# Layer 0's heads turned by DMA instead of TensorE, and a new order inside the period, in a two-layer graph kernel

## The chip, the cores and the metric

The kernel runs on one core of a Trainium2 chip. The time is the device time of one execution in microseconds (us); a kernel's time is the median of its runs. In the profile PE is TensorE (PEld its weight loads), DVE is VectorE, ACT is ScalarE, POOL is GpSimd and SP is SyncE, whose queue issues nearly all DMAs here. A line such as L522 is a line of the kernel's source.

## The reference

There are 64 independent graphs of 256 nodes with 512 features, and a mask `adj` per graph. Two residual layers of masked attention follow each other, each after a layer norm and a relu. Layer 0 has 8 heads and also keeps only pairs of nodes whose mapped features have a cosine over 0.1; layer 1 has 4 heads and an output product.

```python
# --- layer 0 (8 heads of 64) ---
h = relu(layernorm(x))
m = h @ map_w.T + map_b
n = m / |m|  per head                      # unit vectors
cos_adj = (n @ n.T) * ~adj > 0.1
q, k = m @ q_w.T + q_b, m @ k_w.T + k_b
p = softmax(where(adj, -1e10, q @ k.T / 8)) * keep     # keep: by node, ~adj[..., 0]
a = cos_adj * p
Ax = a @ (h @ gcn_map_w.T + gcn_map_b)
out = relu(Ax @ gcn_W.T / (a.sum(-1) + 1))
x = x + out
# --- layer 1 (4 heads of 64) ---
h = relu(layernorm(x))
q, k, v = h @ Wq, h @ Wk, h @ Wv
attn = softmax(where(adj, q @ k.T / 8, -max))
x = x + (attn @ v) @ Wo + bo
```

## The kernel before

The graphs run through a software pipeline. `period(i)` works on four graphs at once: on graph i (called `g`) it does layer 0's attention and the products of layer 1; on graph i-1 (`b`) layer 1's attention and the output; on graph i+1 (`nx`) the map, messages, queries and keys of layer 0; on graph i+2 (`n2`) the input norm and its transpose. On every engine the instructions stand in the order of the source. Inside a period the products are generators (`m` map, `s` messages, `q` queries, `k` keys, `j` layer 1's queries and keys, `v` its values), and each `next` puts one step of their matmuls into the order.

Products of 256-token blocks are made of seven block products each, from sums and differences of the blocks (`left_factors`, on POOL). Attention is kept transposed: scores have keys on partitions and queries along the row. Softmax numerators `e` are masked by DVE and halved into `d` by POOL; sums over keys are matmuls with ones. Layer 0's sums need one more thing: where a pair of nodes is far (`far`, the transposed upper block of cosines), e is set to zero by `far_back`. Layer 0's result `av` has features on partitions and tokens along the row, so it has to be turned before it is added to `x`: in `heads_back`, by eight transposes of TensorE (`p_l`). The input of the first layer is turned in another way: `sent` takes each fp32 number apart into two 16-bit halves, sends both through a DMA transpose (which moves 16-bit elements), and `join` puts the halves back together on ACT.

The helpers that the change touches, or that stand on the way between layer 0's heads and layer 1's norm:

```python
    def shifts(g, tag):

        deviations(g)
        g.shift = small.tile([P, NT], F32, tag="shift", name=f"shift{tag}")
        for t in range(NT):
            nc.scalar.activation(g.shift[:, t:t + 1], g.less[:, t:t + 1], AF.Copy, scale=g.rs[:, t:t + 1])
        g.flat = sb1.tile([P, NT, 2, D], U16, tag="kT", name=f"flat{tag}")
        g.turn = sb1.tile([P, 2, NKC, S], U16, tag="nT", name=f"turn{tag}")

    def sent(g, t):

        bits = g.xn.bitcast(U16).rearrange("p (d k) -> p k d", k=2)
        for k in range(2):
            nc.scalar.copy(g.flat[:, t, k, :], bits[:, k, :])
            nc.sync.dma_start_transpose(out=g.turn[:, k, :, t * P:(t + 1) * P], in_=g.flat[:, t, k, :])

    def join(g, k):
        nc.scalar.copy(g.bits[:, k], g.turn[:, k])

    def lengths(g, p):
        g.rn = sb1.tile([P, S], F32, tag="rn", name=f"rn{g.i}")
        nc.vector.tensor_scalar_max(g.rn, p, COS_EPS * COS_EPS)

    def by_head(rows, step, dst, name):

        n = P // step
        by = dram.tile([n // 2, 2, S], F32, tag=f"by{step}", name=f"by_{name}")
        nc.sync.dma_start(out=by.rearrange("c s q -> (c s) q"), in_=rows[::step, :])
        for s in range(2):
            nc.sync.dma_start(out=dst[s * DH:(s + 1) * DH], in_=by[None, :, s, :].to_broadcast([DH, n // 2, S]))

    def far_back(g, c):

        e = g.e[c][:, :, S:S + P]
        nc.vector.scalar_tensor_tensor(e, g.far[c], 0.0, e, op0=ALU.is_gt, op1=ALU.mult)

    def values(g, n):
        av = bank(f"av{g.i}_{n}")
        for c in (2 * n, 2 * n + 1):
            weighed(av, c - 2 * n, g.sem, g.e[c], 2 * c)
        nc.scalar.activation(g.avs[:, 2 * n:2 * n + 2, :], av, AF.Relu)

    def total(g, sm):
        g.homes = both_homes(g.i)
        g.sms = g.homes[:, 0, :]
        nc.scalar.activation(g.sms, sm, AF.Copy, accum_out=chk[:, g.i, 0:1])

    def sums_back(g):

        rt = bank(f"rt{g.i}", [P, NT, P])
        for t in range(NT):
            nc.tensor.transpose(rt[:, t, :], g.sms[:, t * P:(t + 1) * P], w.ident)
        r = small.tile([P, NT, 2, 4], F32, tag="r", name=f"r{g.i}", bufs=1)
        nc.vector.reciprocal(r, rt.rearrange("p t (k n) -> p t n k", n=32)[:, :, :2, :])
        rc = small.tile([P, NT, 2, 4], F32, tag="rc", name=f"rc{g.i}", bufs=1)
        nc.scalar.activation(rc, r, AF.Copy, accum_out=chk[:, g.i, 1:2])
        g.rk = small.tile([P, NT, H0], F32, tag="rk", name=f"rk{g.i}", bufs=1)
        for t in range(NT):
            nc.vector.tensor_scalar_mul(g.rk[:, t, :], r[:, t].rearrange("p n k -> p (n k)"), g.keep[:, t:t + 1])

    def heads_back(g):
        for t in range(NT):
            p = bank(f"p_l{g.i}_{t}", [P, NKC, P])
            for c in range(NKC):
                nc.tensor.transpose(p[:, c, :], g.avs[:, c, t * P:(t + 1) * P], w.ident)
            o = sb2.tile([P, H0, DH], F32, tag="xn", name=f"o{g.i}_{t}")
            nc.vector.tensor_mul(o, p.rearrange("p c (h d) -> p (c h) d", d=DH),
                                 g.rk[:, t, :, None].to_broadcast([P, H0, DH]))
            nc.gpsimd.tensor_add(g.xs[:, t, :], g.xs[:, t, :], o.rearrange("p h d -> p (h d)"))

    def own(b, home):
        own = sb1.tile([P, 2, NIC, S], F32, tag=home, name=f"own{b.i}")
        b.avs1, b.z = own[:, 0], own[:, 1]

    def sums1(b, parts):

        zb = bank(f"zb{b.i}", [P, S])
        for c in range(NIC):
            ps = parts(c)
            for j, part in enumerate(ps):
                for s in range(2):
                    h = 2 * c + s
                    nc.tensor.matmul(zb[32 * h:32 * (h + 1), :], w.ones[:, :32], part[:, s, :],
                                     start=(j == 0), stop=(j == len(ps) - 1))
        b.rz = sb1.tile([P, S], F32, tag="rz", name=f"rz{b.i}")
        nc.scalar.activation(b.rz, zb, AF.Copy, accum_out=chk[:, b.i, 2:3])

    def inverted(b):

        nc.vector.reciprocal(b.rz, b.rz)
        by_head(b.rz, 32, b.z, f"rz{b.i}")

    def divided(b):
        nc.vector.tensor_mul(b.avs1, b.avs1, b.z)
```

Of the pools: a `tag` names a buffer, and two tiles of one tag with `bufs=1` follow each other in the same memory. `avs`, `sq` and layer 1's `hT` share "wide"; the left factors have "sh"; `sem` has two buffers. All PSUM tiles come in turn from a ring of eight banks.

The period (`turned` makes p_t, `result` makes p_o):

```python
    def period(i):
        g, nx = graphs[i], graphs[i + 1]
        b, n2 = graphs.get(i - 1), graphs.get(i + 2)

        def off_edges(*cs):
            for c in cs:
                masked(g.e[c], g.mask, edges=False)

        def halved_sums(*cs):
            for c in cs:
                g.d[c] = halves(g.e[c], f"0_{i}_{c}")


        if b:
            b.e1 = [exps(products(b.k1T, b.q1T, c, f"sc1_{b.i}_{c}"), f"1_{b.i}_{c}") for c in range(NIC)]
        for c in range(NKC):
            g.e[c] = exps(products(g.kT, g.qT, c, f"sc0_{i}_{c}"), f"0_{i}_{c}")
        if b:
            for c in range(NIC):
                masked(b.e1[c], b.mask, edges=True)
        m, s = mapped(nx), messages(nx)
        next(m)
        next(s)

        off_edges(0, 1)
        halved_sums(1, 0)
        if b:
            b.d1 = [halves(b.e1[c], f"1_{b.i}_{c}") for c in range(NIC)]
        units(g)
        next(m)
        off_edges(2)
        halved_sums(2)
        next(m)
        next(s)
        next(m)

        for c in range(NKC):
            far_off(g, c, cosines(g, c))
            if c == 0:
                off_edges(3)
                halved(nx, lambda: halved_sums(3))
        for c in range(NKC):
            far_added(g, c, 0)
        if n2:
            shifts(n2, f"0_{n2.i}")
        q = queries(nx)
        next(q)
        next(s)
        if n2:
            scaled(n2, f"0_{n2.i}", 0)
        next(q)
        if n2:
            sent(n2, 0)
        squares(nx)
        next(s)
        if n2:
            scaled(n2, f"0_{n2.i}", 1)
            sent(n2, 1)
        for c in range(NKC):
            if c < 3:
                next((q, s, q)[c])
            far_back(g, c)
            far_added(g, c, 1)
        lengths(nx, norms(nx))

        if b:
            sums1(b, lambda c: [b.d1[c]])
            own(b, "qk1")
            inverted(b)
            nc.scalar.copy(b.avs1, values1(b))
        g.avs = sb1.tile([P, NKC, S], F32, tag="wide", name=f"avs{i}")
        values(g, 0)
        values(g, 1)
        total(g, sums(g, lambda c: [g.d[c]], "sm"))
        if n2:
            joined(n2, f"0_{n2.i}")
            join(n2, 0)
        k = keys(nx)
        next(k)
        if b:
            nc.scalar.activation(b.rz, b.rz, AF.Copy, accum_out=chk[:, b.i, 3:4])
        sums_back(g)
        heads_back(g)
        if n2:
            join(n2, 1)
        next(k)
        if n2:
            edges(n2, g.homes)
        if b:
            divided(b)
        moments(g, f"1_{i}")
        next(k)
        deviations(g)
        normalized(g, f"1_{i}")
        nc.scalar.activation(nx.rn, nx.rn, AF.Sqrt)

        nc.scalar.activation(spare[:, 1:], spare[:, :1], AF.Exp)
        if b:                                   # p_o
            for t in range(NT):
                result(b, t)
            nc.sync.dma_start(out=out_t[b.i], in_=b.xs)
        if i + 3 < B:
            graphs[i + 3] = load(i + 3)
        g.h1T = turned(g, f"1_{i}", "wide")
        j = queries_keys1(g)
        for t in range(NT):
            nc.gpsimd.tensor_add(g.xs[:, t, :], g.xs[:, t, :], w.bo_b)
        next(k)
        next(j)
        v = values_in(g)
        next(v)
        nc.vector.reciprocal(nx.rn, nx.rn)
        spread(nx)
        ...  # the other steps of j and v; left_factors of n2.hT; moments of graph i + 3
```

(Cut here: the loads, the general fallback kernel that is compiled but isn't entered with these inputs, the first graph's preparation, and `closing`, which treats the last two graphs without the pipeline and also calls `values`, `heads_back`, `sums1` and `inverted`.)

Of the kernel before, what the change touches and what calls it, by code (L numbers as in the profile page):

```python
# [150 lines left out]
def fast_path(ctx, tc, a, w, chk, out):  # L151
# [232 lines left out]
    def by_head(rows, step, dst, name):  # L384

        n = P // step
        by = dram.tile([n // 2, 2, S], F32, tag=f"by{step}", name=f"by_{name}")
        nc.sync.dma_start(out=by.rearrange("c s q -> (c s) q"), in_=rows[::step, :])
        for s in range(2):
            nc.sync.dma_start(out=dst[s * DH:(s + 1) * DH], in_=by[None, :, s, :].to_broadcast([DH, n // 2, S]))  # L390

    def spread(g):

        g.nT = sb1.tile([P, NKC, S], F32, tag="nT", name=f"nT{g.i}")
        by_head(g.rn, 16, g.nT, f"rn{g.i}")
# [109 lines left out]
    def sums_back(g):  # L505
# [85 lines left out]
    def sums1(b, parts):  # L591
# [26 lines left out]
    def period(i):  # L618
# [21 lines left out]
        next(s)  # L640

# [6 lines left out]
        off_edges(2)  # L648
        halved_sums(2)
# [33 lines left out]
        if b:  # L683
            sums1(b, lambda c: [b.d1[c]])
            own(b, "qk1")
            inverted(b)
            nc.scalar.copy(b.avs1, values1(b))
        g.avs = sb1.tile([P, NKC, S], F32, tag="wide", name=f"avs{i}")
        values(g, 0)
        values(g, 1)  # L690
        total(g, sums(g, lambda c: [g.d[c]], "sm"))
        if n2:
            joined(n2, f"0_{n2.i}")
            join(n2, 0)
# [5 lines left out]
        heads_back(g)  # L700
        if n2:
            join(n2, 1)
        next(k)
        if n2:
# [19 lines left out]
        g.h1T = turned(g, f"1_{i}", "wide")  # L724
        j = queries_keys1(g)
# [16 lines left out]
    def closing():  # L742
# [24 lines left out]
        values(g, 0)  # L767
        values(g, 1)
# [9 lines left out]
        if b:  # L778
            sums1(b, lambda c: both(b.e1[c]))
            own(b, "kT")  # L780
# [7 lines left out]
        if b:  # L788
            inverted(b)
        g.h1T = turned(g, f"1_{g.i}", "wide")  # L790
# [409 lines left out]
```

## Time and profile before

| | |
|---|---|
| time, median of 3 runs | 3622.2 us (3621.92 to 3622.47) |
| span in the profiled run | 3620.2 us |
| granted TensorE clock, mean | 0.998 |
| busy: PE, PEld | 3594.1 us (99%), 3133.2 us (87%) |
| busy: DVE, ACT, POOL | 2625.7 us (73%), 1971.2 us (54%), 2222.5 us (61%) |
| DMA | 191.65 MB in 359208 packets, mean 53 GB/s |
| p_l (L522), the transposes of layer 0's heads | 512 matmuls, 66.4 us busy |
| DMA transposes on SP: far, turn, mask | 256, 248, 128 |

Busy time is the time in which an engine had at least one instruction under way. Matmuls are pipelined, so the mean duration of one is longer than the distance between two; in a timeline, the difference of two starts tells what a group takes of the engine. A timeline line has the start, the duration, the engine, the source line, the operation, output and inputs, and the count; in brackets stands the idle time of the engine before it, with what ended that idle time. A line of waits has the total in us, how often it happened, and the longest. The chain of work that ended last is followed back from the last instruction, and its shares say which engine set the end.

### The profile page before, as it was taken

The page shows a single profiled execution, that of the slowest core. Times are in us where ns is not written, and L with a number is a line of the kernel's source. Part 1 is how long each engine was busy: PE and PEld are TensorE (multiplying, and loading weights), DVE is VectorE, ACT ScalarE, POOL GpSimd, SP SyncE. Part 2 cuts the span into 40 slices and gives each one's busy share as a digit, 9 for nine tenths or more (in the row PEclk, how much of TensorE's full clock was granted, in tenths as well). Part 3 has the DMA queues.
Part 4 walks back from the last instruction along what each step waited for, and adds up shares of the span by engine and source line. Part 5 has one row for each costly group of instructions (what it writes and reads, how often), then busy time and mean ns, then how long its engine had stood idle before and what let it go on. Part 6 is the DMA issues. An engine that isn't in the chain of part 4 may idle for free.

```text
span 3620.2 us, 79022 instructions
## 1 busy us (share of the span) xinstructions
PE 3594.1 (99%) x29945; PEld 3133.2 (87%) x29945; DVE 2625.7 (73%) x5549; ACT 1971.2 (54%) x4796; POOL 2222.5 (61%) x2044
## 2 busy tenths in 40 slices
PE   8999999999999999999999999999999999999998
PEld 7888888889888888888888988888889888888896
DVE  7777767777777777776777777767777777777776
ACT  4555555555555555555555555555555555555553
POOL 4656666566566665665656656666566566665662
PEclk9999999999999999999999999999999999999999
DMA  4121121212211212112122121121111211211111
GB/s 119 42 61 44 54 57 47 55 46 54 61 44 52 54 48 58 44 55 61 42 55 52 49 60 44 54 56 47 55 46 54 61 44 53 57 47 57 45 48 34
DMA packets 359208, 191.65 MB, mean 53 GB/s; under 512 B 270348, under 2 KB 325160, under 8 KB 358824
## 3 DMA queue, kind: packets, MB, share of 16 engines
q1 hardware_dynamic: 358088, 185.97, 19.4%
q8 instruction: 240, 3.93, 0.5%
q14 instruction: 144, 1.18, 0.1%
q10 hardware_dynamic: 544, 0.52, 0.0%
q0 software_dynamic: 192, 0.04, 0.0%
HBM read 94.41 MB, written 34.34 MB: 36 GB/s over the span
## 4 chain that ended last, share of the span: by engine, by line
PE 98%; DVE 1%; ACT 0%; issue 0%; DMA 0%; POOL 0%; SPq 0%; DVEq 0%; ACTq 0%; POOLq 0%
PE sc L416 10%; PE av L443 9%; PE p_m L287 7%; PE p_q L287 7%; PE p_k L287 7%; PE p_qk L287 6%; PE p_s L282 6%; PE p_o L615 6%; PE co L453 5%; PE p_qk_z L287 5%; PE p_m_z L287 5%; PE p_q_z L287 5%; PE p_k_z L287 5%; PE p_s_z L282 5%; PE p_v L545 3%; PE p_v_z L545 2%
## 5 line engine op out<-in xcount | busy, mean ns | idle before, releaser
L436 POOL TENSOR_TENSOR d<-e 128x512 f32<-128x512 f32 x376 | 585.8, 1584 | 297.9 <-DVE e L432 297.9
L472 POOL TENSOR_TENSOR d<-d,e 128x512 f32<-128x512 f32 x504 | 635.5, 1281 | 155.4 <-DVE e L477 155.4
L264 POOL TENSOR_TENSOR sh<-hT 128x256 f32<-128x256 f32 x128 | 93.5, 731 | 533.8 <-ACT hT L220 284.0
L423 ACT ACTIVATE e<-sc 128x512 f32<-128x512 f32 x768 | 383.3, 647 | 61.3 <-POOL sh L265 56.3
L526 POOL TENSOR_TENSOR xs<-xs,o 128x512 f32<-128x512 f32 x128 | 188.5, 1494 | 354.1 <-DVE o L524 354.1
L432 DVE TENSOR_TENSOR e<-e,mask 128x1024 f32<-128x1024 f32 x256 | 364.3, 1443 | 0.5 <-ACT e L423 0.5
L466 DVE SCALAR_TENSOR_TENSOR e<-co,e 128x256 f32<-128x256 f32 (+1 forms) x1024 | 282.3, 348 | 35.6 <-ACT up L463 35.6
L463 ACT ACTIVATE up<-co,below 128x128 bf16<-128x128 f32 x512 | 160.3, 365 | 182.8 <-PE co L453 177.4
L416 PE MATMUL sc<-qT,kT 64*128 64x256 f32 x2048 | 233.7, 376 | 0.0
L443 PE MATMUL av<-e,sem 128*64 128x256 f32 x2048 | 232.4, 379 | 0.2 <-DVE e L477 0.2
L615 PE MATMUL p_o<-wo,own 128*128 128x512 f32 x512 | 230.8, 593 | 0.0
L416 PEld LDWEIGHTS sc<-qT,kT 64*128 64x128 f32 x2048 | 220.2, 187 | 1.4 <-ACT hT L220 0.3
L443 PEld LDWEIGHTS av<-e,sem 128*64 128x64 f32 x2048 | 146.7, 137 | 75.2 <-DVE e L477 1.1
L511 DVE RECIPROCAL r<-rt 128x16 f32<-128x16 f32 x64 | 16.5, 258 | 268.5 <-PE rt L509 268.5
L197 DVE BATCH_NORM_STATS2 st<-xs 128x6 f32<-128x512 f32 x256 | 173.9, 679 | 26.8 <-POOL xs L526 23.2
L477 DVE SCALAR_TENSOR_TENSOR e<-far,e 128x256 f32<-128x256 bf16 x256 | 190.5, 764 | 0.7 <-DMA far<-up 0.7
L453 PE MATMUL co<-nT 64*128 64x256 f32 (+1 forms) x2048 | 185.0, 330 | 0.0
L453 PEld LDWEIGHTS co<-nT 64*128 64x128 f32 x2048 | 161.4, 187 | 19.5 <-issue 0.4
L615 PEld LDWEIGHTS p_o<-wo,own 128*128 128x128 f32 x512 | 92.3, 190 | 92.9 <-issue 91.6
L252 ACT COPY hT<-turn 128x1024 uint16<-128x1024 uint16 x124 | 167.4, 1350 | 0.0
L727 POOL TENSOR_TENSOR xs<-xs,bo_b 128x512 f32<-128x512 f32 x126 | 157.6, 1273 | 0.0
L483 ACT ACTIVATE avs<-av 128x512 f32<-128x512 f32 x128 | 76.5, 598 | 145.7 <-PE av L443 145.7
(242 smaller groups left out, 9459.2 us busy)
## 6 DMA issues: line engine op xcount, KB each, us to landing
xs<-in_x_dram SPq DMA_DIRECT2D x64, 512.0 KB
nT<-by_rn SPq DMA_DIRECT2D x128, 256.0 KB
out_dram<-xs SPq DMA_DIRECT2D x63, 512.0 KB
own<-by_rz SPq DMA_DIRECT2D x126, 128.0 KB
ad<-in_adj_dram SPq DMA_DIRECT2D x64, 64.0 KB
far<-up SPq DMA_TRANSPOSE x256
turn<-flat SPq DMA_TRANSPOSE x248
mask<-homes SPq DMA_TRANSPOSE x128
```

Source lines behind the costliest of these rows:

```text
L282: nc.tensor.matmul(region, src[:, c, :], wt[:, block, c, :], start=p not in opened, stop=True, skip_group_check=True)
L287: nc.tensor.matmul(region[:, f, :], wt[:, block, c, f * P:(f + 1) * P], src[:, c, :], start=p not in opened, stop=True, skip_group_check=True)
L416: nc.tensor.matmul(ps[s][:, j, :], rows[h, c, j * P:(j + 1) * P], cols[h, c, :], start=True, stop=True)
L423: nc.scalar.activation(e[:, s, :], p.rearrange("p j q -> p (j q)"), AF.Exp, scale=SCALE)
L432: nc.vector.tensor_mul(e, e, m)
L436: nc.gpsimd.tensor_add(d, e[:, :, :S], e[:, :, S:])
L443: nc.tensor.matmul(av[s * DH:(s + 1) * DH, n, :], vs[:, j, (h0 + s) * DH:(h0 + s + 1) * DH], q[:, s, j * S:(j + 1) * S], start=(j == 0), s ...
L453: nc.tensor.matmul(ps[s][:, j, j * P:], g.nT[h, c, j * P:(j + 1) * P], g.nT[h, c, j * P:], start=(j == 0), stop=True, skip_group_check=True)
L466: nc.vector.scalar_tensor_tensor(e, p.rearrange("p j q -> p (j q)")[:, lo:hi], THRESHOLD, e, op0=ALU.is_gt, op1=ALU.mult)
L472: nc.gpsimd.tensor_add(g.d[c], g.d[c], g.e[c][:, :, half * S:(half + 1) * S])
L477: nc.vector.scalar_tensor_tensor(e, g.far[c], 0.0, e, op0=ALU.is_gt, op1=ALU.mult)
L615: nc.tensor.matmul(p, b.avs1[:, c, t * P:(t + 1) * P], w.wo1[:, c, :], start=(c == 0), stop=(c == NIC - 1))
```

## The change

Layer 0's heads no longer pass through TensorE on their way back to tokens by features. In the periods (not in `closing`), `values` leaves `av` in PSUM; `heads_sent` copies its 16-bit halves out of PSUM on ACT, without the relu, and sends each half of each pair of feature blocks through a DMA transpose; `heads_joined` puts the halves together on ACT, into the buffer of `sem`, which is free once `av` has been computed; `heads_added` does relu and scaling in one DVE instruction and adds the result to `x` on POOL.

The order in the period is new so that the trip has other work of TensorE beside it: layer 1's sums and the norm matmuls come right after the first step of the queries, layer 1's reciprocals are sent off earlier, layer 0's attention comes before layer 1's, then the last step of the queries, and then layer 0's sums and the keys. Smaller moves go with it: the square root of graph i+2's deviations moves to the head of the period, the joins of its input move behind the heads and behind `turned`, and the check sum of layer 1's sums (`summed_up`) is taken in PSUM after its reciprocal instead of before it.

```diff
--- before.py
+++ after.py
@@ -226,7 +226,6 @@
 
     def shifts(g, tag):
 
-        deviations(g)
         g.shift = small.tile([P, NT], F32, tag="shift", name=f"shift{tag}")
         for t in range(NT):
             nc.scalar.activation(g.shift[:, t:t + 1], g.less[:, t:t + 1], AF.Copy, scale=g.rs[:, t:t + 1])
... (by_head is split in two: sent_by_head sends the rows to DRAM, by_head spreads them from there)
@@ -480,7 +484,27 @@
         av = bank(f"av{g.i}_{n}")
         for c in (2 * n, 2 * n + 1):
             weighed(av, c - 2 * n, g.sem, g.e[c], 2 * c)
+        return av
+
+    def unsigned(g, n, av):
         nc.scalar.activation(g.avs[:, 2 * n:2 * n + 2, :], av, AF.Relu)
+
+    def heads_sent(g, n, av):
+
+        bits = av.bitcast(U16).rearrange("p c (q k) -> p k c q", k=2)
+        if n == 0:
+            g.heads = sb1.tile([P, 2, NKC, NT, P], U16, tag="sh", name=f"heads{g.i}")
+        for k in range(2):
+            flat = g.avs[:, 2 * n + k, :].bitcast(U16)
+            nc.scalar.copy(flat.rearrange("p (c q) -> p c q", q=S), bits[:, k])
+            nc.sync.dma_start_transpose(out=g.heads[:, k, 2 * n:2 * n + 2].rearrange("p c t f -> p (c t) f"), in_=flat)
+
+    def heads_joined(g, n):
+
+        bits = g.sem.bitcast(U16).rearrange("p t (c f k) -> p k c t f", k=2, f=P)
+        c = slice(2 * n, 2 * n + 2)
+        for k in range(2):
+            nc.scalar.copy(bits[:, k, c], g.heads[:, k, c])
 
     def sums(g, parts, name):
 
@@ -514,6 +538,12 @@
         g.rk = small.tile([P, NT, H0], F32, tag="rk", name=f"rk{g.i}", bufs=1)
         for t in range(NT):
             nc.vector.tensor_scalar_mul(g.rk[:, t, :], r[:, t].rearrange("p n k -> p (n k)"), g.keep[:, t:t + 1])
+
+    def heads_added(g, t):
+        o = sb2.tile([P, H0, DH], F32, tag="xn", name=f"o{g.i}_{t}")
+        nc.vector.scalar_tensor_tensor(o, g.sem[:, t, :].rearrange("p (h d) -> p h d", d=DH), 0.0,
+                                       g.rk[:, t, :, None].to_broadcast([P, H0, DH]), op0=ALU.max, op1=ALU.mult)
+        nc.gpsimd.tensor_add(g.xs[:, t, :], g.xs[:, t, :], o.rearrange("p h d -> p (h d)"))
 
     def heads_back(g):
         for t in range(NT):
@@ -598,13 +628,19 @@
                     h = 2 * c + s
                     nc.tensor.matmul(zb[32 * h:32 * (h + 1), :], w.ones[:, :32], part[:, s, :],
                                      start=(j == 0), stop=(j == len(ps) - 1))
+        b.zb = zb
+
+    def summed_up(b):
+        nc.scalar.activation(b.zb, b.zb, AF.Copy, accum_out=chk[:, b.i, 2:3])
+
+    def inverted(b):
+
         b.rz = sb1.tile([P, S], F32, tag="rz", name=f"rz{b.i}")
-        nc.scalar.activation(b.rz, zb, AF.Copy, accum_out=chk[:, b.i, 2:3])
-
-    def inverted(b):
-
-        nc.vector.reciprocal(b.rz, b.rz)
-        by_head(b.rz, 32, b.z, f"rz{b.i}")
+        nc.vector.reciprocal(b.rz, b.zb)
+        b.by = sent_by_head(b.rz, 32, f"rz{b.i}")
+
+    def spread_inverses(b):
+        by_head(b.by, b.z)
 
     def divided(b):
         nc.vector.tensor_mul(b.avs1, b.avs1, b.z)
@@ -638,6 +674,8 @@
         m, s = mapped(nx), messages(nx)
         next(m)
         next(s)
+        if n2:
+            nc.scalar.activation(n2.rs, n2.rs, AF.Sqrt)
 
         off_edges(0, 1)
         halved_sums(1, 0)
@@ -646,6 +684,8 @@
         units(g)
         next(m)
         off_edges(2)
+        if n2:
+            nc.vector.reciprocal(n2.rs, n2.rs)
         halved_sums(2)
         next(m)
         next(s)
@@ -658,49 +698,58 @@
                 halved(nx, lambda: halved_sums(3))
         for c in range(NKC):
             far_added(g, c, 0)
+        squares(nx)
         if n2:
             shifts(n2, f"0_{n2.i}")
+            scaled(n2, f"0_{n2.i}", 0)
         q = queries(nx)
-        next(q)
-        next(s)
-        if n2:
-            scaled(n2, f"0_{n2.i}", 0)
         next(q)
         if n2:
             sent(n2, 0)
-        squares(nx)
-        next(s)
-        if n2:
             scaled(n2, f"0_{n2.i}", 1)
-            sent(n2, 1)
-        for c in range(NKC):
-            if c < 3:
-                next((q, s, q)[c])
-            far_back(g, c)
-            far_added(g, c, 1)
-        lengths(nx, norms(nx))
-
         if b:
             sums1(b, lambda c: [b.d1[c]])
             own(b, "qk1")
             inverted(b)
+        p_n = norms(nx)
+        next(s)
+        if n2:
+            sent(n2, 1)
+        if b:
+            spread_inverses(b)
+            summed_up(b)
+        next(q)
+        lengths(nx, p_n)
+        for c in range(2):
+            far_back(g, c)
+            far_added(g, c, 1)
+        next(s)
+        next(q)
+        for c in range(2, NKC):
+            far_back(g, c)
+            far_added(g, c, 1)
+        next(s)
+
+        g.avs = sb1.tile([P, NKC, S], F32, tag="wide", name=f"avs{i}")
+        for n in range(2):
+            heads_sent(g, n, values(g, n))
+        if b:
             nc.scalar.copy(b.avs1, values1(b))
-        g.avs = sb1.tile([P, NKC, S], F32, tag="wide", name=f"avs{i}")
-        values(g, 0)
-        values(g, 1)
+        next(q)
         total(g, sums(g, lambda c: [g.d[c]], "sm"))
+        for n in range(2):
+            heads_joined(g, n)
+        k = keys(nx)
+        next(k)
+        if b:
+            nc.scalar.activation(b.rz, b.rz, AF.Copy, accum_out=chk[:, b.i, 3:4])
+        sums_back(g)
+        heads_added(g, 0)
         if n2:
             joined(n2, f"0_{n2.i}")
             join(n2, 0)
-        k = keys(nx)
         next(k)
-        if b:
-            nc.scalar.activation(b.rz, b.rz, AF.Copy, accum_out=chk[:, b.i, 3:4])
-        sums_back(g)
-        heads_back(g)
-        if n2:
-            join(n2, 1)
-        next(k)
+        heads_added(g, 1)
         if n2:
             edges(n2, g.homes)
         if b:
@@ -722,6 +771,8 @@
         if i + 3 < B:
             graphs[i + 3] = load(i + 3)
         g.h1T = turned(g, f"1_{i}", "wide")
+        if n2:
+            join(n2, 1)
         j = queries_keys1(g)
         for t in range(NT):
             nc.gpsimd.tensor_add(g.xs[:, t, :], g.xs[:, t, :], w.bo_b)
... (closing: values is followed by unsigned, sums1 by summed_up, inverted by spread_inverses)
```

More of the change, by code (lines that the diff above doesn't have):

```diff
@@ L382, in lengths, with sent_by_head @@
         nc.vector.tensor_scalar_max(g.rn, p, COS_EPS * COS_EPS)
-    def by_head(rows, step, dst, name):
+    def sent_by_head(rows, step, name):
         n = P // step
@@ L388, in by_head @@
         nc.sync.dma_start(out=by.rearrange("c s q -> (c s) q"), in_=rows[::step, :])
+        return by
+    def by_head(by, dst):
         for s in range(2):
-            nc.sync.dma_start(out=dst[s * DH:(s + 1) * DH], in_=by[None, :, s, :].to_broadcast([DH, n // 2, S]))
+            nc.sync.dma_start(out=dst[s * DH:(s + 1) * DH],
+                              in_=by[None, :, s, :].to_broadcast([DH, by.shape[0], S]))
     def spread(g):
         g.nT = sb1.tile([P, NKC, S], F32, tag="nT", name=f"nT{g.i}")
-        by_head(g.rn, 16, g.nT, f"rn{g.i}")
+        by_head(sent_by_head(g.rn, 16, f"rn{g.i}"), g.nT)
     def units(g):
@@ L686, in period @@
             inverted(b)
+        p_n = norms(nx)
[20 more added lines that the diff above has]
+        if b:
             nc.scalar.copy(b.avs1, values1(b))
-        g.avs = sb1.tile([P, NKC, S], F32, tag="wide", name=f"avs{i}")
-        values(g, 0)
-        values(g, 1)
+        next(q)
         total(g, sums(g, lambda c: [g.d[c]], "sm"))
-        if n2:
-            joined(n2, f"0_{n2.i}")
-            join(n2, 0)
+        for n in range(2):
+            heads_joined(g, n)
         k = keys(nx)
@@ L699, in period @@
         sums_back(g)
-        heads_back(g)
+        heads_added(g, 0)
         if n2:
-            join(n2, 1)
+            joined(n2, f"0_{n2.i}")
+            join(n2, 0)
         next(k)
+        heads_added(g, 1)
         if n2:
@@ L766, in closing @@
         g.avs = sb1.tile([P, NKC, S], F32, tag="wide", name=f"avs{g.i}")
-        values(g, 0)
-        values(g, 1)
+        for n in range(2):
+            unsigned(g, n, values(g, n))
         nc.scalar.activation(spare[:, 1:], spare[:, :1], AF.Sqrt)
@@ L779, in closing @@
             sums1(b, lambda c: both(b.e1[c]))
+            summed_up(b)
             own(b, "kT")
@@ L789, in closing @@
             inverted(b)
+            spread_inverses(b)
         g.h1T = turned(g, f"1_{g.i}", "wide")
```

## The prediction

> **What bounds the kernel now.** I read the page first: the busy shares and the chain that ended last.
>
> ```profile
> PE 3594.1 (99%) x29945; PEld 3133.2 (87%) x29945; DVE 2625.7 (73%) x5549; ACT 1971.2 (54%) x4796; POOL 2222.5 (61%) x2044
> ...
> PE 98%; DVE 1%; ACT 0%; issue 0%; DMA 0%; POOL 0%; SPq 0%; DVEq 0%; ACTq 0%; POOLq 0%
> ```
>
> TensorE is the end-setting engine and there is nothing beside it: 98% of the chain is matmuls. So the time is the sum of TensorE's work plus its waits. The list of waits, for TensorE alone, shows how few waits there are:
>
> ```profile
> PE p_t L219 <- DVE xn L210: 13.2, 3, 8.5
> ...
> PE av L443 <- DVE e L477: 0.2, 1, 0.2
> ```
>
> Three waits in 64 graphs. One of 8.5 us is the start; the timeline puts one of 2.26 us in the first period and one of 2.49 us in the closing part. In the steady state TensorE waits for nobody. From this follow two rules for the prediction: what is taken from TensorE is gained in full, and what makes it wait is lost in full.
>
> The timeline of TensorE over one steady period (start, duration with the overlap to the next group):
>
> ```profile
> 1525.65 3.62 PE L443 MATMUL av<-e,sem 128*64 128x256 f32 x32
> 1529.20 1.07 PE L493 MATMUL sm<-d,two 128*32 128x256 f32 x16
> 1530.20 2.05 PE L287 MATMUL p_k<-mT,wk 128*128 128x128 f32 x16
> 1532.09 0.38 PE L509 MATMUL rt<-ident,homes 128*128 128x128 f32 x2
> 1532.31 1.04 PE L522 MATMUL p_l<-ident,avs 128*128 128x128 f32 x8
> 1533.18 1.06 PE L287 MATMUL p_k_z<-mT,wk 128*128 128x128 f32 x8
> ...
> 1536.75 3.60 PE L615 MATMUL p_o<-wo,own 128*128 128x512 f32 x8
> 1540.19 1.04 PE L219 MATMUL p_t<-ident,xn 128*128 128x128 f32 x8
> ```
>
> Durations overlap, so cost is read from start to start: p_l (the eight transposes that turn layer 0's heads back) costs 1533.18 - 1532.31 = 0.87 us. A whole period is 55.86 us (p_q starts at 1512.06 and again at 1567.92). Last, the other engines in the same period, between the heads and p_t:
>
> ```profile
> 1533.14 1.29 DVE L524 TENSOR_TENSOR o<-p_l,rk 128x512 f32<-128x512 f32 x2
> ...
> 1533.91 2.96 POOL L526 TENSOR_TENSOR xs<-xs,o 128x512 f32<-128x512 f32 x2 [5.26 <-DVE o L524]
> ...
> 1536.90 0.69 DVE L197 BATCH_NORM_STATS2 st<-xs 128x6 f32<-128x512 f32 x1 [0.34 <-POOL xs L526]
> ...
> 1538.91 1.00 DVE L210 TENSOR_SCALAR xn<-xs,mv,rs 128x512 f32<-128x512 f32 x2
> ```
>
> The reader is to see a chain beside TensorE: heads scaled (o), added to x (POOL), moments, normalized rows xn, which p_t needs. The first xn is done near 1539.4 and the second at 1539.9; p_t starts at 1540.19. The slack is about 0.7 us for the first row tile and, p_t's first half taking 0.44, also 0.7 for the second. It is hidden, with less room than the 0.87 us that is to be removed from TensorE ahead of p_t.
>
> **What the Trainium skill says.** "VectorE: DVE Perf Modes", section "The three transpose paths", gives 390 ns for a 128x128 transpose on TensorE and 1309 ns through DMA: a longer path, but on an engine that isn't the bound. The trace agrees on the second: a DMA transpose of 128x512 16-bit elements holds the SP queue 1257 ns (turn<-flat, median); on TensorE 273 ns is one transpose's latency and 0.109 us its pitch here. "DMA: Bandwidth & Descriptors", section "Anatomy of one DMA", puts a fixed cost of some 2 us on every DMA, mostly until completion is seen. The trace's only wait on a DMA transpose agrees: in the closing part the last one (far<-up) is issued at 3573.6 and its reader starts at 3575.97, 2.4 us. "GPSIMD Engine Reference", in the table that opens it, says that GpSimd's SBUF interface is shared with VectorE instructions that have two SBUF inputs. The trace agrees: xs<-xs,o takes 1267 ns at least and 1742 at most, and in the period above the slow one is the one beside own<-own.
>
> **The change, part by part.**
>
> *Removed from TensorE:* the 8 p_l transposes of each of 63 periods (the closing part keeps its own): 0.87 us a period, 54.8 us in all. That is 1.5%, the whole possible gain but for one trifle: the last step of p_q is preceded in the list of waits of the weight loads by 11.3 us over 63 times (for uup_q), and the start p_q_z to p_n takes 1.03 instead of 0.89. In the new order that step comes after both attentions, long after its input is there: 0.14 us more.
>
> *Added elsewhere:* the two 0.60 us avs relu copies of ACT become four 16-bit copies out of PSUM (estimated 0.6 each, as avs has the same 512 elements a row), and four joining copies into sem. Two flat copies of 512 16-bit elements together take 1.14 us, so 0.57 each. ACT gains 1.2 + 2.3 = 3.5 us per period, from 54% to about 60%. SP gains four transposes of 1.26 us. DVE's o reads SBUF instead of PSUM at about the same 0.69 us.
>
> *Does attention now wait?* Layer 0's av starts earlier: 1525.65 less layer 1's av (1.78) and the last p_q step (1.03) = 1522.84; its third and fourth quarters read e at about 1524.6 and 1525.5. DVE must finish far_back by then, and now has the 1.74 us reciprocal of layer 1's sums ahead of it. DVE's far work ends at 1516.04, the reciprocal at 17.8, the sem, qT and rn pieces (0.33 each) at 19.2, two far_backs (0.73 for two) at 20.6. The next pieces follow p_q's middle step, which ends at 1521.97 (1520.97 plus zb and p_n, 1.0, now ahead of it); two pieces to 22.8, the last far_backs at 23.5 and 24.3. Both are over 1 us early. No wait.
>
> *The heads' path.* All that stood ahead of sm still does, so sm ends at the same 1530.2. av's halves end at about 1524.6 and 1526.4; copies to 1525.9 and 1527.7; the four transposes on SP from 1525.4, one after another, to 1530.4; the last lands 2.4 us after its issue at 1529.15, so at 1531.6. ACT takes the sums first (homes, done 1530.7 as now), then the four joins: 4 x 0.57 = 2.3, to 1533.0 or, with a dearer pattern of 0.62, to 1533.2. The last transpose lands before its join starts: DMA isn't what gates, ACT behind sm is. So o starts at 1533.1 to 1533.3, against 1533.14 now: the chain doesn't move, while TensorE comes 0.87 us sooner.
>
> *From there to p_t.* kT's first piece now stands between the two o's, and o and own both have two SBUF inputs beside the POOL adds, so the first add is likely to take 1.7 to 1.9: 1533.9 to 1535.7; the second 1.27 more, 1537.0 to 1537.1, against 1536.87 now. From there to the first xn it's 2.5 us as now: 1539.5 to 1539.7. TensorE reaches p_t at 1540.19 - 0.87 = 1539.32. Besides, p_o wants own at 1535.88; own starts after the second o (1534.9) and ends at 1535.9 to 1536.1. Both waits overlap in part: a p_o that starts late arrives late at p_t. I take 0.4 us in all.
>
> *Sum:* each of 62 periods gains 0.87 + 0.14 - 0.40 = 0.61 us, 37.8 in all. The first period, which waits at p_t already, gains nothing and may lose 1 us. 3622.2 - 37.8 + 1 = 3585.
>
> **The rivals.**
>
> *All hidden:* no wait at p_t or p_o. For it: my chain has only some 0.2 to 0.4 us over, within its errors. Against it: the slack before (0.7) is smaller than what is removed (0.87), and no part of the chain gets shorter. It'd make 3622.2 - 62 x 1.01 = 3560.
>
> *The DMA round trip gates:* if transposes queue behind by_rz's spread or land 2 us later than estimated, the last join, both o's and p_t move by more than 1 us a period. For it: SP holds ten transposes a period in a row and the reply time is seen only once. Against it: 0.8 us between landing and use. Each us costs 62: 3620 or more.
>
> *ACT becomes a bound locally:* the joins push back u2p_k, hT and u5p_k. The first hT join moves 2.3 us; u5p_k is then at 1536.1, where it is now, and the second hT join goes into a hole of 2 us after h1T. I expect no cost; if wrong, uup_k and p_t are late by the same, 0.5 us a period, 3610.
>
> *A bad order elsewhere*, as p_n before its squares: sq ends at about 1513.9 and p_n starts at 1514.5. No wait expected.
>
> **Range and chances.** The range is that of the wait: from 0.04 us (3562) to 0.75 us a period (3606). Over 2% faster needs less than 3551, more than TensorE sheds; over 2% slower, above 3694, needs 1.8 us of new waiting a period. I give 3% each.
>
> **What would show it.** Right: p_l falls from 512 matmuls to 8; a period near 55.25 us; TensorE waits 0.2 to 0.6 us, about 62 times, for xn at p_t or own at p_o; SP's last heads transpose lands before its join begins; o starts near 2.9 us after sm ends. Wrong: no such waits (then 3560); sem joins that wait for DMA; av waiting for far_back; or TensorE work other than p_l that changes its pitch with the new neighbours.

## The result, and the profile after

The changed kernel takes 3674.5 us against 3622.3: ratio 1.0145, 95% interval 1.0128 to 1.0163. It is slower by 52 us, 0.83 us in each of 63 periods. 3585 was predicted, with a range that ended at 3606.

The page of the changed kernel, busy shares and the chain that ended last:

```profile
PE 3590.6 (98%) x29441; PEld 3082.7 (84%) x29441; DVE 2677.3 (73%) x5549; ACT 2164.6 (59%) x5174; POOL 2234.5 (61%) x2044
...
PE 86%; DVE 5%; ACT 4%; DMA 2%; issue 2%; POOL 0%; DVEq 0%; SPq 0%; POOLq 0%
```

TensorE lost 504 matmuls, as it should. But the chain, 98% TensorE before, now leaves TensorE for 14% of the span. The waits of TensorE, matmuls and then weight loads (total us, times, longest):

```profile
PE p_o L651 <- DVE own L646: 48.9, 61, 1.1
PE p_t L219 <- DVE xn L210: 15.6, 4, 8.3
```

```profile
PEld p_t L219 <- PE p_o L651: 53.0, 62, 1.2
```

Before, p_t waited three times and little else waited at all. Now p_o waits in 61 periods for own, and p_t's weight loads stand behind p_o in all 62. The last line is not what it seems: p_o is only the last thing that the profile saw end. The timelines of one period tell what p_t waited for. First TensorE:

```profile
1607.62 1.16 PE L286 MATMUL p_q_z<-sm,wq 128*128 128x128 f32 x8
1608.71 1.07 PE L517 MATMUL sm<-d,two 128*32 128x256 f32 x16
1609.71 2.05 PE L286 MATMUL p_k<-mT,wk 128*128 128x128 f32 x16
...
1614.50 1.06 PE L286 MATMUL p_k_z<-sm,wk 128*128 128x128 f32 x8
1616.22 3.67 PE L651 MATMUL p_o<-wo,own 128*128 128x512 f32 x8 [0.67 <-DVE own L646]
1619.94 1.08 PE L219 MATMUL p_t<-ident,xn 128*128 128x128 f32 x8
```

and the other engines beside it:

```profile
1610.22 2.63 ACT L507 COPY sem<-heads 128x512 uint16<-128x512 uint16 x4
...
1612.88 0.69 DVE L544 SCALAR_TENSOR_TENSOR o<-sem,rk 128x512 f32<-128x512 f32 x1 [0.21 <-ACT sem L507]
...
1613.65 1.27 POOL L546 TENSOR_TENSOR xs<-xs,o 128x512 f32<-128x512 f32 x1 [7.60 <-DVE o L544]
...
1613.82 1.65 DVE L544 SCALAR_TENSOR_TENSOR o<-sem,rk 128x512 f32<-128x512 f32 x1
...
1615.40 0.68 DVE L646 TENSOR_TENSOR own<-own 128x512 f32<-128x512 f32 x1
...
1615.55 1.65 POOL L546 TENSOR_TENSOR xs<-xs,o 128x512 f32<-128x512 f32 x1 [0.63 <-DVE o L544]
...
1617.24 0.69 DVE L197 BATCH_NORM_STATS2 st<-xs 128x6 f32<-128x512 f32 x1 [0.34 <-POOL xs L546]
...
1619.25 1.00 DVE L210 TENSOR_SCALAR xn<-xs,mv,rs 128x512 f32<-128x512 f32 x2
```

Two instructions of one shape, on the same engine, take 0.69 and 1.65 us. The second o starts 0.17 us after POOL's first add and ends 0.55 us after it. With own and the second add it is the other way round: own starts 0.15 us before that add and keeps its 0.68, and the add takes 1.65. So the one that starts second is held up: the o ends 0.55 us after the add, the second add 1.12 us after own. All 63 second o's and all 62 such own's of this trace show the same. own is behind the second o, so p_o is late; the second add is behind it too, so the first xn ends at 1619.25 + 0.54 (xn's own duration before the change) = 1619.79, and p_t starts 0.15 later. Undelayed, TensorE would have been at p_t at 1614.50 + 0.89 + 3.44 = 1618.83: 1.1 us are lost here. In the period before this one, p_k_z starts at 1557.47 and p_t at 1563.44, so by the same sum 1.6.

A second loss is not a wait at all. From the start of p_q to the start of sm TensorE took 1529.20 - 1512.06 = 17.14 us before, and 1608.71 - 1591.22 = 17.49 now, with the same matmuls in another order: 0.35 us. These are also the medians over all periods. Where the 0.35 us lie stands under experiment 7.

### The profile page after: what moved, and what is told of

Read it like the earlier page. It is cut to its first block, busy times and chain, and to the rows that moved or that the text cites. A ratio compares the mean times of both kernels' runs of the same rounds, so it can differ in the third digit from the quotient of the medians.

```text
span 3673.2 us, 78457 instructions
## 1 busy us (share of the span) xinstructions
PE 3590.6 (98%) x29441; PEld 3082.7 (84%) x29441; DVE 2677.3 (73%) x5549; ACT 2164.6 (59%) x5174; POOL 2234.5 (61%) x2044
## 4 chain that ended last, share of the span: by engine, by line
PE 86%; DVE 5%; ACT 4%; DMA 2%; issue 2%; POOL 0%; DVEq 0%; SPq 0%; POOLq 0%
PE sc L420 9%; PE av L447 9%; PE p_q L286 7%; PE p_m L286 6%; PE p_o L651 6%; PE p_qk L286 6%; PE p_s L281 6%; PE co L457 5%; PE p_s_z L281 5%; PE p_qk_z L286 5%; PE p_m_z L286 5%; PE p_q_z L286 5%; PE p_v L575 3%; ACT sem L507 3%; DVE o L544 3%; PE p_v_z L575 2%
## 5 line engine op out<-in xcount | busy, mean ns | idle before, releaser
L476 POOL TENSOR_TENSOR d<-d,e 128x512 f32<-128x512 f32 x504 | 651.5, 1325 | 27.9 <-DVE e L481 27.9
L499 ACT COPY avs<-av 128x512 uint16<-128x512 uint16 x252 | 135.3, 589 | 285.8 <-PE av L447 285.8
L311 DVE TENSOR_TENSOR qT<-p_q_z,u5p_q 128x256 f32<-128x256 f32 x64 | 27.2, 425 | 279.6 <-PE p_q_z L286 279.6
L481 DVE SCALAR_TENSOR_TENSOR e<-far,e 128x256 f32<-128x256 bf16 x256 | 202.7, 830 | 1.6 <-DMA far<-up 1.5
L507 ACT COPY sem<-heads 128x512 uint16<-128x512 uint16 x252 | 169.5, 761 | 9.0 <-DMA heads<-avs 8.6
```

The costliest lines, as they stand in the source:

```text
L476: nc.gpsimd.tensor_add(g.d[c], g.d[c], g.e[c][:, :, half * S:(half + 1) * S])
L507: nc.scalar.copy(bits[:, k, c], g.heads[:, k, c])
```

## The theories and the experiments

**Theory 1:** the loss is the chain from the joins on ACT through the two o's, own and GpSimd's adds to xn, grown longer above all by the second o beside GpSimd, plus 0.35 us of TensorE's spacing. **Theory 2:** the new order itself costs. **Theory 3:** the trip through DMA costs. In the comparisons below the kernel before took 3622 to 3623 us beside each.

**1. The new order, with TensorE's transposes.**

```diff
-            heads_sent(g, n, values(g, n))
+            unsigned(g, n, values(g, n))
-        for n in range(2):
-            heads_joined(g, n)
-        heads_added(g, 0)        # and heads_added(g, 1)
+        heads_back(g)
```

> The new order kept, layer 0's heads turned by TensorE again. Theory 1 (the loss is the chain joins on ACT, two o's on DVE with GpSimd beside them, adds, norm, in front of p_t): chain gone, what is left of the change is TensorE's wider spacing between new neighbours, 0.35 us a period read from the timelines: 3622 + 22 = 3644 us. Theory 2 (the new order itself costs): the 0.87 us of transposes come on top of the changed kernel, 3674 + 55 = 3729. Theory 3 (the round trip of the transposes through DMA): as theory 1, 3622 to 3644.

Measured: 3643.9 us, ratio 1.0059 (1.0042 to 1.0076). The waits at p_o are gone, and p_t's line is like that of the kernel before (13.2 us, three times):

```profile
PE p_t L219 <- DVE xn L210: 13.1, 3, 8.4
```

So the order costs 21 us by itself, as the spacing says, and is not the main loss. Theory 2 falls as the whole cause. With the 54.8 us of transposes off, a kernel without waits in this order would take 3643.9 - 54.8 = 3589; the changed one is 85 us above it. That is what remains to be explained.

**2. The factors rk stay in PSUM.** rk is written into free columns of the bank that holds rt, so o reads one operand from SBUF and one from PSUM.

```diff
-        g.rk = small.tile([P, NT, H0], F32, tag="rk", name=f"rk{g.i}", bufs=1)
+        g.rk = rt[:, :, H0:2 * H0]       # in the last graph as before
```

> One thing changed in the new kernel: the scale factors rk stay in PSUM, so that o has one SBUF input instead of two. Theory 1: the second o, 1.65 us beside a GpSimd add, goes back to 0.69; own ends 0.95 earlier, the wait of p_o for own goes, the first row tile of xn comes 0.7 earlier: 0.7 x 62 = 43 us less, 3631. Theories 2 and 3: no change, 3674.

Measured: 3638.0 us, ratio 1.0044 (1.0027 to 1.0061), 36 us less than the changed kernel. The two o's by their line (minimum, median, maximum in ns):

```profile
L547 DVE SCALAR_TENSOR_TENSOR o<-sem,rt x126: 676/683/690, 79.2 to 3561.2; 128x512 f32<-128x512 f32 x126
```

In the changed kernel this line has 691/1158/1658. No o is slow any more, with the adds still beside the second one. own, which has two SBUF operands, now starts 0.77 us after the first add and takes 1.06 us, and the second add, which starts inside own, takes 1.72: again the later one of each pair is held up. One operand's place was worth 36 us.

**3. own ahead of the heads.**

```diff
         next(q)
+        if b:
+            divided(b)
         total(g, sums(g, lambda c: [g.d[c]], "sm"))
...
-        if b:
-            divided(b)
         moments(g, f"1_{i}")
```

> One thing changed: own<-own (layer 1's division) goes ahead of the heads on DVE, into a hole of over 2 us. Theory 1: p_o no longer waits, but p_t is held by xn all the same; xn comes some 0.37 us earlier: 23 us less, 3651. If the wait of p_o for own is the loss itself: 49 us less, 3625. Theories 2 and 3: no change, 3674.

Measured: 3646.6 us, ratio 1.0067 (1.0050 to 1.0084), 28 us less. The wait at p_o is gone and the one at p_t shows in its own name, now that p_o no longer starts late:

```profile
PE p_t L219 <- DVE xn L210: 56.6, 65, 8.3
```

That is the true releaser of p_t: xn, not p_o. The 49 us in the list for p_o weren't the loss; they overlapped with the later wait.

**4. Two joins ahead of the sums' copy on ACT.**

```diff
+        heads_joined(g, 0)
         total(g, sums(g, lambda c: [g.d[c]], "sm"))
-        for n in range(2):
-            heads_joined(g, n)
+        heads_joined(g, 1)
```

> One thing changed: the first two joins go ahead of the sums' copy on ACT, where ACT waits for sm. Theory 1: o starts 0.2 us earlier in periods where no join waits for DMA (rk is the next to gate it), up to 0.9 where one does: about 0.3 x 62 = 19 us less, 3655. Theory 3: what the joins wait for DMA is 8.6 us in all and is not shortened, 3674. Theory 2: 3674.

Measured: 3664.3 us, ratio 1.0117 (1.0100 to 1.0134): 10 us less, half of what I expected. ACT's joins gate, but little is to be had in front of them, for the joins then catch up with their transposes. Total us, times and longest of ACT's waits at that line:

```profile
ACT sem L507 <- DMA heads<-avs: 50.8, 77, 2.0
```

In the changed kernel they waited 8.6 us, 18 times.

**5. The old order, with the heads by DMA.** The kernel before with `heads_sent` in place of the relu copies, the joins behind the sums and `heads_added` in place of `heads_back`; the joins of graph i+2's input stand as in the changed kernel.

```diff
         g.avs = sb1.tile([P, NKC, S], F32, tag="wide", name=f"avs{i}")
-        values(g, 0)
-        values(g, 1)
+        for n in range(2):
+            heads_sent(g, n, values(g, n))
         total(g, sums(g, lambda c: [g.d[c]], "sm"))
+        for n in range(2):
+            heads_joined(g, n)
```

> The other part alone: the old order, with layer 0's heads turned by DMA. Layer 0's attention then ends 2.8 us later before the sums, and the four transposes follow by_rz and its spread on SP. Theory 1 (the new order hides the DMA trip; what remains is the chain behind the joins): o starts some 3 us later than in the changed kernel, joins wait for DMA in nearly every period; 3674 - 22 + 3 x 62 = about 3840 us. Theory 2 (the order is what costs): 3622 - 55 + at most 20, under 3600.

Measured: 4052.4 us, ratio 1.1184 (1.1159 to 1.1210). The direction is theory 1's, and the size is well beyond it. The joins do wait for DMA:

```profile
ACT sem L503 <- DMA heads<-avs: 303.4, 187, 5.5
```

and TensorE waits 285 us at p_k_z, for the first piece of kT is late there: its input u2p_k stands behind the joins on ACT, and kT itself behind the first o on DVE. A further part of the excess over my estimate shows in the windows of one period: the wait, the matmuls right after it, and p_o (window, length, busy us and count by engine, granted clock, DMA share, GB/s):

```profile
1514.80:1519.10 4.30, 0.00 (x0) 0.00 (x0) 1.08 (x3) 3.27 (x8) 0.31 (x1) 0.83 0.27 61
1519.10:1521.30 2.20, 2.08 (x8) 1.78 (x8) 2.20 (x3) 2.20 (x7) 1.57 (x2) 0.50 0.01 4
1521.30:1526.40 5.10, 5.04 (x9) 2.24 (x10) 4.17 (x11) 2.00 (x4) 1.80 (x3) 0.69 0.12 26
```

In finer windows the granted clock is 1.00 from 1514.80 to 1517.60 and 0.50 from 1517.70 to 1524.40: it is halved 2.8 us into the wait and stays so for nearly 7 us, over p_k_z and more than half of p_o. Over the whole run its mean is 0.95, against 0.998 in the changed kernel. So, as built here, the trip needs the new order: in the old one the kernel takes a further 378 us.

**6. The three repairs together.** The edits of 2, 3 and 4 in one kernel.

> Three repairs of the chain together (rk in PSUM, own early, the first two joins early), TensorE's order as in the changed kernel. Theory 1: from 3638 (rk in PSUM alone) own no longer lies beside the second add, 0.4 us a period, and o starts 0.16 us earlier: 3603 us; a wait of p_t for xn of some 0.2 us is left. If the single gains simply add up: 3674 - 36 - 28 - 10 = 3600. Floor without any wait: 3622 - 55 + 22 = 3589.

Measured: 3607.8 us, ratio 0.9959 (0.9944 to 0.9974), faster than the kernel before. The single gains (36, 28, 10) would add up to 74; together they are 67. The chain is the loss, for shortening it at three places removes four fifths of the 85 us. What makes up the last fifth isn't shown.

**7. The sums ahead of the last queries step.** Experiment 1 with the sums moved ahead of the last queries step.

```diff
-        next(q)
         total(g, sums(g, lambda c: [g.d[c]], "sm"))
+        next(q)
```

> TensorE's spacing alone: the kernel with the new order and TensorE transposes (3644), with layer 0's sums moved ahead of the last step of the queries. If the 0.35 us a period are paid where 32-column matmuls and full-width matmuls meet, two such borders go (queries to sums 0.2, attention to queries 0.05) and none comes: 0.25 x 62 = 15 us less, 3628. If they are paid for another reason (waits for buffers, DVE), no change: 3644.

Measured: 3631.4 us, ratio 1.0025 (1.0015 to 1.0036), 12.5 us less than experiment 1. TensorE's timeline:

```profile
1532.81 1.07 PE L517 MATMUL sm<-d,two 128*32 128x256 f32 x16
1533.81 1.16 PE L286 MATMUL p_q_z<-sm,wq 128*128 128x128 f32 x8
1534.81 1.95 PE L286 MATMUL p_k<-mT,wk 128*128 128x128 f32 x16
1536.60 0.38 PE L533 MATMUL rt<-ident,homes 128*128 128x128 f32 x2
1536.81 1.04 PE L552 MATMUL p_l<-ident,avs 128*128 128x128 f32 x8
1537.69 1.06 PE L286 MATMUL p_k_z<-mT,wk 128*128 128x128 f32 x8
1538.58 1.61 PE L286 MATMUL p_k<-sm,wk 128*128 128x128 f32 x13
```

From start to start, p_q_z took 1608.71 - 1607.62 = 1.09 us ahead of sm in the changed kernel; here, behind sm, they take 1534.81 - 1533.81 = 1.00, and p_k_z, with full-width neighbours on both sides, 1538.58 - 1537.69 = 0.89. The first keys step stood right behind sm there and took 1611.60 - 1609.71 = 1.89 to the start of the next group, rt; here it stands behind the q step and takes 1536.60 - 1534.81 = 1.79. sm took 1.00 both times. So about 0.1 us was paid at each of two places beside the 32-column sm, 0.19 us a period, and 12.5 us / 62 = 0.20 was gained.

These two aren't the 0.35 us, though. The kernel before paid one of them too: its first keys step, behind sm, took the same 1532.09 - 1530.20 = 1.89. Where the 0.35 us lie is read from the two timelines. Before:

```profile
1512.06 2.05 PE L287 MATMUL p_q<-mT,wq 128*128 128x128 f32 x16
1513.94 1.03 PE L282 MATMUL p_s_z<-wc,hT 128*128 128x256 f32 x4
1514.81 1.89 PE L282 MATMUL p_s<-wc,sh 128*128 128x256 f32 x8
```

and in the changed kernel:

```profile
1591.22 2.05 PE L286 MATMUL p_q<-mT,wq 128*128 128x128 f32 x16
1593.20 0.64 PE L629 MATMUL zb<-d,ones 128*32 128x256 f32 x8
...
1594.20 1.13 PE L281 MATMUL p_s_z<-wc,hT 128*128 128x256 f32 x4
1595.17 1.89 PE L281 MATMUL p_s<-wc,sh 128*128 128x256 f32 x8
...
1601.33 1.03 PE L281 MATMUL p_s_z<-wc,sh 128*128 128x256 f32 x4
1602.29 3.67 PE L447 MATMUL av<-e,sem 128*64 128x256 f32 x32
```

The 32-column zb and p_n now stand between full-width steps: p_q ahead of them takes 1.98 instead of 1.88, the first p_s_z behind them 0.97 instead of 0.87. The last p_s_z, now ahead of the 64-column av, takes 0.96 instead of 0.87, and the last queries step, now between av and sm, 1.09 instead of 1.03. That is 0.10 + 0.10 + 0.09 + 0.06 = 0.35; all else between p_q and sm adds up to the same time. No run moves zb and p_n alone.

**8. Heads by DMA with the sums first.** rk in PSUM; sums, then the last queries step, own, and the transposes of the sums ahead of the keys; both o's ahead of the first piece of kT.

```diff
-        next(q)
         total(g, sums(g, lambda c: [g.d[c]], "sm"))
+        next(q)
+        if b:
+            divided(b)
         for n in range(2):
             heads_joined(g, n)
+        sums_back(g)
         k = keys(nx)
         next(k)
...
-        sums_back(g)
         heads_added(g, 0)
+        heads_added(g, 1)
```

> The three repairs' aim by another order: rk in PSUM; layer 0's sums ahead of the last queries step and their transposes ahead of the keys, own ahead of them on DVE, and both o's ahead of the first piece of kT. Theory 1: sums are no longer what gates the joins; the last DMA landing is (1.3 us after it was); o still starts near 1.5 us earlier relative to the keys, both adds end 2 us earlier, no wait is left at p_t: 3622 - 55 + 22 - 15 = 3574 us. If the landing of the transposes comes later than thought, up to 0.5 us a period more: 3605.

Measured: 3596.0 us, ratio 0.9925 (0.9908 to 0.9943), the fastest of all. What is left of waits beyond start and end:

```profile
PE p_k_z L286 <- DVE kT L311: 13.8, 18, 1.7
```

In these periods the last join waits for its transpose (1.57 us in one of them) and the pieces behind it on ACT and DVE, kT among them, are late. With 3631.4 - 54.8 = 3577 as the figure without waits in this order, 19 us are still lost.

**9. The trip left out.** The joins read the flat halves, no transposes are issued. The heads are not turned back: this kernel leaves that out.

```diff
-            nc.sync.dma_start_transpose(out=g.heads[:, k, ...], in_=flat)
...
-            nc.scalar.copy(bits[:, k, c], g.heads[:, k, c])
+            nc.scalar.copy(bits[:, k, c], flat)     # flat: g.avs[:, 2 * n + k, :] as 16 bits
```

> The changed kernel without the DMA transposes of the heads: the joins read the flat halves directly, so that this kernel's features are not turned back (it leaves the turning out); all else stays. What it saves is what the DMA trip costs where it now stands. Theory 1 (the chain behind the joins is the loss, DMA gates some of the periods): the joins' 8.6 us of waits go and little more, 3666 us. Theory 3 (the DMA trip is the loss): all waits at p_o and p_t go, 3622 - 55 + 22 = 3589.

Measured: 3663.3 us, ratio 1.0115 (1.0098 to 1.0132). The whole trip is worth 11 us where it stands; 41 us of waits at p_o stay:

```profile
PE p_o L649 <- DVE own L644: 41.0, 61, 0.8
```

Theory 3 falls.

**10. The heads' adds on DVE.**

```diff
-        nc.gpsimd.tensor_add(g.xs[:, t, :], g.xs[:, t, :], o.rearrange("p h d -> p (h d)"))
+        nc.vector.tensor_add(g.xs[:, t, :], g.xs[:, t, :], o.rearrange("p h d -> p (h d)"))
```

> The changed kernel with the heads' two adds on DVE instead of GpSimd, so that nothing on GpSimd lies beside the second o, which keeps its two SBUF inputs. If o is slow only beside a GpSimd add: both o's take 0.69 us, none 1.65. If it is slow for another reason (sem just written by ACT, the operand rk): 1.65 stays. The time moves little either way, DVE then does both adds in a row (4 x 0.69 and own): first xn about where it is, 3660 to 3674 us.

Measured: 3694.0 us, ratio 1.0196 (1.0179 to 1.0213). All o's, still with two SBUF operands:

```profile
L544 DVE SCALAR_TENSOR_TENSOR o<-sem,rk x126: 681/688/694, 79.2 to 3617.9; 128x512 f32<-128x512 f32 x126
```

So neither the operands nor the data alone make o slow, but a GpSimd add beside it. With 2 this settles the mechanism from both sides. My time was wrong: the adds now stand ahead of kT and own on DVE, and p_k_z waits for kT 24 times (16.5 us) where it waited 5 times (1.7 us), beside 52.5 us at p_o.

**11. Attention earlier still.** Experiment 8 with the queries' fourth step moved behind the sums and the messages' last step between the two halves of the attention.

```diff
-        next(q)
         for c in range(2, NKC):
             far_back(g, c)
             far_added(g, c, 1)
-        next(s)
...
             heads_sent(g, n, values(g, n))
+            if n == 0:
+                next(s)
...
         next(q)
+        next(q)
```

> The kernel of the eighth experiment (3596) with layer 0's attention earlier still: the queries' fourth step goes behind the sums, the messages' last step between the two halves of the attention, so that the first two transposes start 1.7 us earlier and the last one about 0.9. Theory 1: the joins no longer wait for DMA and p_k_z no longer for kT (13.8 us in 18 periods, and as much again in small change): 3596 - 22 + up to 6 for two more borders of narrow matmuls = 3578. If the attention now waits for far_back: 0.3 us a period more, 3600.

Measured: 3651.1 us, ratio 1.0080 (1.0063 to 1.0097): wrong by 73 us, and neither of my cases.

```profile
PE p_q_z L286 <- DVE uup_q L331: 36.5, 63, 0.9
```

The waits for kT are gone, but two queries steps now stand side by side. The second writes the bank that DVE (uup_q) has yet to read after the first. In one period they start at 1540.22 and 1541.95, 1.73 us apart, where such a step behind sm took 1.00 in experiment 7: 0.73 x 62 = 45 us. Taking it off would leave 3651 - 45 = 3606, an estimate no better than experiment 8, so nothing here says that an earlier attention gains.

## Why the prediction was wrong, point by point

- *TensorE sets the end; 54.8 us of transposes go.* Right: p_l fell to 8 matmuls, and in the median period TensorE takes 13.65 us from sm to the first p_qk in experiment 7 and 12.78 in experiment 8, which has the same matmuls there but for the transposes: 0.87 less.
- *The last queries step saves 0.14 us a period.* Wrong in sign. I put its 1.03 us down to a wait for uup_q. In the changed kernel its input is there long before, and it takes 1.09, now ahead of the 32-column sm instead of the 32-column p_n. I had read one border in one place and not counted the new ones: TensorE's spacing grew by 0.35 us, and experiment 1 measures 21 us of loss where the sum had 8.7 of gain.
- *Attention doesn't wait for far_back.* Right: one wait of 0.3 us in the whole run.
- *DMA isn't what gates, ACT behind sm is.* Right in the main: the trip is worth 11 us (experiment 9). The 1.26 us for which a transpose holds the queue is not its whole trip, and the landing was taken too short: the last join starts at 1555.59 in a period in which SP ended its issues at 1552.87; 2.7 us after the issue's end, where the reader in the closing part came 1.1 after it. 18 joins waited, 8.6 us in all.
- *o starts at 1533.1 to 1533.3.* On that clock (cosines at 1588.40 instead of 1509.24, so 79.16 off) it starts at 1533.72. 0.35 of it is the spacing, which TensorE shares.
- *From there to p_t; "I take 0.4 us in all".* This is the step that failed. I had the places right, own at p_o and xn at p_t, and named the shared interface. But I let GpSimd's add suffer (1.7 to 1.9 us) and kept o at 0.69. It was the other way round: the add took 1.27 and the second o, which starts inside it, 1.65, and own and the second add stand behind that o. own ended at 1536.92 instead of 1535.9 to 1536.1, the first xn at 1540.63 instead of 1539.5 to 1539.7. The loss is 85 us / 62 = 1.4 us a period instead of 0.4. The trace before held the warning, in the same period and beside the two adds, of which the first starts at 1533.91:

```profile
1534.68 1.06 DVE L610 TENSOR_TENSOR own<-own 128x512 f32<-128x512 f32 x1
```

own, which takes 0.68 where nothing holds it up, starts inside the first add here, takes 1.06 and ends 0.55 us after it. I read only what own did to the second add, not what the first add did to own.

So the place of the loss was seen, and two terms of the sum failed: the wait before p_t, where the wrong engine was taken to be held up, and the spacing, which had the wrong sign. Mine was -53.9 - 8.7 + 24.8 + 1 = -37; measured it is -54.8 + 21.6 + 85.4 = +52, with 3643.9 - 3622.3 = 21.6 for the order and 3674.5 - 3589.1 = 85.4 for the chain. Of the rivals, only the number of the one that puts the loss on the DMA trip, 3620 or more, takes in the outcome. That is luck: the trip was the smallest part. ACT as a local bound (3610; the sum of 3585 and 62 x 0.5 us is 3616) hardly showed: p_k_z waited 1.7 us in all for kT. TensorE had no wait at p_n.

Shown by runs: the cost of the order, of the operand, of own's place and of the trip. Read from the timelines and not tested by a run of its own: how the 0.35 us divide.

## What to carry to other kernels

Work moved off the bounding engine is gained only as far as the chain beside it has slack: write that chain down instruction by instruction before and after, and ask of each which neighbour it now shares an interface with. Of a VectorE instruction with two SBUF operands and a GpSimd add, the one that started second was held up here, so ask which starts first, keep one of the operands in PSUM, or put nothing on GpSimd beside it. And when steps are reordered, count the borders between full-width and narrow matmuls (a run shows it for 32 columns, the timelines also for 64), and keep two steps that reuse one PSUM bank apart.

## What the runs showed of the hardware that was not expected

- Of a VectorE instruction with two SBUF operands and a GpSimd add that overlap, the one that started first kept its time, and the other ended a fixed time after it. In the changed kernel the second o, started 0.17 us after the add, took 1.65 us instead of 0.69 and ended 0.55 us after the add, which kept its 1.27; own, begun 0.15 us before the second add, kept 0.68, and that add took 1.65 and ended 1.12 us after own. In experiment 2 own, begun 0.77 us after the first add, took 1.06 and ended 0.55 us after it; the second add began while own ran, took 1.72 and ended 1.13 us after own. With one operand in PSUM, o took 0.68 beside the add.
- Eight 128x128 matmuls took 1.09 us from start to start between a 64-column and a 32-column group, 1.00 behind the 32-column one, 0.89 among their like (p_k_z in experiment 7).
- In a wait of 4.3 us TensorE's granted clock fell to 0.50 after 2.8 us and stayed there for nearly 7 us (one period of experiment 5): the mean p_o matmul took 824 ns in that run, 602 in the changed kernel.
